# Two steps of a scan's beginning from GpSimd to VectorE, its pieces between the convolution products, and more buffers for x

## The chip, the cores and the metric

The kernel runs on one core of one Trainium2 chip. The metric is the device time of one execution in microseconds (us), the median of several runs. Short names as in the profile: PE is TensorE (PEld its weight loads), DVE VectorE, ACT ScalarE, POOL GpSimd, SP SyncE, whose queue issues all DMA transfers here.

## The reference

Input x is (4, 64, 64, 96) in fp32. Two layers hold a selective scan over the pixels (layers 0 and 1), two hold attention and a small feed-forward net (layers 2 and 3). The change concerns the scan layers only. Cut to what matters, one of them computes:

```python
x = x + conv_ref(_gn(x), ...)          # _gn: group norm, 32 groups of 3 channels

xz = einsum('bhwc,ec->bhwe', x, in_proj_w)             # 96 -> 2 * 192
xp, z = split(xz, 2)
xc = silu(depthwise_conv_3x3(xp) + conv_b)             # 192 channels
xs = [rows, columns, rows reversed, columns reversed]  # K = 4 directions over 4096 pixels
dts, B, C = split(xs @ x_proj_weight, [6, 22])         # rank 6, 16 states, 16 states
delta = softplus(dts @ dt_projs_weight + bias)
h = exp(delta * A) * h + (delta * u) * B               # scan along the pixels, u = xs
y = sum over states(h * C) + D * u
out = (layernorm(sum over directions(y)) * silu(z)) @ out_proj_w
```

## The kernel before

**Units.** A scan layer is worked on in two pairs of images, so there are four units (two layers, two pairs). The 2 x 192 channels of a pair lie in three tiles of 128 partitions (j = 0, 1, 2; tile 2 holds the last 64 channels of both images). Before each unit's scan stands a stage `between_scans` (L107), which makes the scan's inputs (`scan_inputs`, L122) and at the same time the outputs of the unit before (`scan_outputs`, L246); the first stage has no outputs to make. Both are generators: for each of the 16 groups of `scan_outputs` (256 pixels of both images) `scan_inputs` is advanced twice.

**The inputs of a scan, in program order.** `measure` (L174) for each of the two images: eight tiles xt of x, 96 x 512, are loaded by SP and go through bn_stats on DVE (L180); two tiny matmuls gm and gv (L187, L195) and a power on POOL (L81) give mean and factor of each group. `project` (L198), eight times for each image: a tile xn of x is loaded (L204), normalised on DVE (L205), multiplied on PE by in_proj (ips, three matmuls, L209); ACT copies the results into padded images img (L211, L212) or puts the gates through Silu into zs (L215, L216), which SP stores to zg. Then the 3x3 convolution, part of it on PE (`conv_product`, L147: nine matmuls cps with diagonal weights for eight rows, then Silu on ACT, L154) and part of it on DVE (`conv_chain`, L158: nine steps L167 and L169 for sixteen rows, then Silu on ACT, L170). Two chains are begun during the projection of the second image; two products stand before the scan's beginning and six products and six chains after it.

**The beginning of a scan.** `PairScan.begin` (L362) does for the first chunk of 1024 pixels what the scan does for later chunks while it runs. `project` (L373) makes B, C and the ranks of delta: six matmuls xps (L390), copies to cdt on ACT (L392), a store of cdt to crow in DRAM (L393), transposes btps (L397). B is then split into three bf16 terms, each the remainder of the one before: parts[0] on ACT (L403), rest on DVE (L404), parts[1] on ACT (L406), parts[2] on POOL (L408), transposes bpps (L412) and a copy to bparts on ACT (L416). `discretise` (L419) makes delta: matmuls dps (L434), Softplus on ACT (L438), du = delta * u on POOL (L440), transposes dups of it (L447), copies to dut on ACT (L449). Both are generators, whose yields mark places where the running scan takes up the next piece. In the stage ahead `begin` exhausts both at once:

```python
conv_product(1, 0)
conv_product(1, 8)
scan.begin(nc, pp)
yield
for n in range(2, 8):
    conv_product(*((1, 8 * n) if n < 6 else (0, 8 * n)))
```

**The order of the work.** In the stages a scheduler of the language orders each engine's instructions from their program order and its own idea of durations when the kernel is built; each engine then works through its list in order and waits where an input or a buffer isn't ready. In the scan itself (`PairScan.scan`, through `InOrder`) the program order is kept; the profile shows all that runs through that helper, the token layers not among it, as L71.

**Buffers.** Tiles with a name share a fixed number of places: two for xt and two for xn; the pool of the stage has three for what names no number. A transfer into a place waits until the tile that was there has been read. Tiles of the scan take over the memory of the stage's tiles, so its first tiles wait for the last of these.

Of the kernel before, what the change touches and what calls it, by code (L numbers as in the profile page):

```python
# [16 lines left out]
F32 = mybir.dt.float32  # L17
# [4 lines left out]
ALU = mybir.AluOpType  # L22
# [6 lines left out]
C = 96  # L29
# [46 lines left out]
def rstd_of(nc, pool, var, shape, tag, half):  # L76

    ve = pool.tile(shape, F32, name=f"{tag}_ve")
    nc.vector.tensor_scalar(ve, var, EPS, None, ALU.add)  # L79
    rs = pool.tile(shape, F32, name=f"{tag}_rs")  # L80
    nc.gpsimd.tensor_tensor(rs, ve, half, ALU.pow)  # L81
    return rs
# [39 lines left out]
def scan_inputs(tc, stage, cst, ident, half, u, scan, layer, pr):  # L122


    nc = tc.nc
    par, zg, x_src = layer.par, layer.zg[pr], layer.x_src
    pa = stage.enter_context(tc.tile_pool(name="a", bufs=1))
    p2 = stage.enter_context(tc.tile_pool(name="a2", bufs=3))
    pp = stage.enter_context(tc.tile_pool(name="a_ps", bufs=5, space=PSUM))

    wi = pa.tile([C, 2, 2 * DI], F32, name="wi")
    nc.sync.dma_start(out=wi, in_=layer.w["wi"].rearrange("i c d -> c i d"))

    diag = pa.tile([128, 9, 128], F32, name="diag")
    for tap in range(9):
        nc.gpsimd.tensor_scalar(diag[:, tap], ident, par[:, 0, P_CONV + tap : P_CONV + tap + 1], None, ALU.mult)

    imgs = []
    for j in range(3):
        img = pa.tile([128, HW + 2, HW + 2], F32, name=f"img{j}", tag=f"img{j}")  # L140
        nc.gpsimd.memset(img[:, 0], 0.0)
        nc.gpsimd.memset(img[:, HW + 1], 0.0)
        nc.gpsimd.memset(img[:, 1 : HW + 1, 0:1], 0.0)
        nc.gpsimd.memset(img[:, 1 : HW + 1, HW + 1 : HW + 2], 0.0)
        imgs.append(img)

    def conv_product(j, c):  # L147

        ps = pp.tile([128, 8, HW], F32, name="cps", tag="mm")
        for tap in range(9):  # L150
            dy, dx = divmod(tap, 3)
            v = imgs[j][:, c + dy : c + dy + 8, dx : dx + HW]
            nc.tensor.matmul(ps, diag[:, tap], v, start=(tap == 0), stop=(tap == 8))
        nc.scalar.activation(  # L154
            u[j][:, HW * c : HW * (c + 8)], ps.rearrange("p h w -> p (h w)"), AF.Silu, bias=par[:, 0, P_CB : P_CB + 1]
        )

    def conv_chain(j, c):  # L158

        s, cols = j // 2, slice(HW * c, HW * (c + 16))  # L160
        to = u[j][:, cols].rearrange("p (h w) -> p h w", w=HW)
        for tap in range(9):
            dy, dx = divmod(tap, 3)
            v = imgs[j][:, c + dy : c + dy + 16, dx : dx + HW]
            weight = par[:, s, P_CONV + tap : P_CONV + tap + 1]
            if tap == 0:
                nc.vector.tensor_scalar(to, v, weight, par[:, s, P_CB : P_CB + 1], ALU.mult, ALU.add)  # L167
            else:
                nc.vector.scalar_tensor_tensor(to, v, weight, to, ALU.mult, ALU.add)  # L169
        nc.scalar.activation(u[j][:, cols], u[j][:, cols], AF.Silu)  # L170

    norms = []

    def measure(i):  # L174

        stats = p2.tile([C, 8, 6], F32, name="stats")
        for g in range(8):
            xt = p2.tile([C, 512], F32, name="xt", bufs=2)
            nc.sync.dma_start(out=xt, in_=x_src[2 * pr + i, :, 512 * g : 512 * g + 512])
            nc.vector.bn_stats(stats[:, g], xt)  # L180
            if g % 2:
                yield
        mv = p2.tile([C, 2], F32, name="mv")
        nc.vector.bn_aggr(mv, stats.rearrange("c g s -> c (g s)"))

        gm = pp.tile([C, 1], F32, name="gm", tag="mm")
        nc.tensor.matmul(gm, cst["group"], mv[:, 0:1], start=True, stop=True)  # L187
        mean = p2.tile([C, 1], F32, name="mean")
        nc.vector.tensor_copy(mean, gm)
        dev = p2.tile([C, 1], F32, name="dev")  # L190
        nc.vector.tensor_tensor(dev, mv[:, 0:1], mean, ALU.subtract)
        spread = p2.tile([C, 1], F32, name="spread")
        nc.vector.scalar_tensor_tensor(spread, dev, dev, mv[:, 1:2], ALU.mult, ALU.add)
        gv = pp.tile([C, 1], F32, name="gv", tag="mm")
        nc.tensor.matmul(gv, cst["group"], spread, start=True, stop=True)  # L195
        norms.append((mean, rstd_of(nc, p2, gv, [C, 1], "gn", half[:C, 0:1])))

    def project(i, c):  # L198


        mine, other = slice(D1 * i, D1 * i + D1), slice(D1 - D1 * i, 128 - D1 * i)
        cols, rows = slice(512 * c, 512 * c + 512), slice(1 + 8 * c, 9 + 8 * c)
        xn = p2.tile([C, 512], F32, name="xn", bufs=2)
        nc.sync.dma_start(out=xn, in_=x_src[2 * pr + i, :, cols])  # L204
        nc.vector.tensor_scalar(xn, xn, *norms[i], ALU.subtract, ALU.mult)  # L205
        pss = []
        for q in range(3):
            ps = pp.tile([128, 8, HW], F32, name=f"ips{q}", tag="mm")
            nc.tensor.matmul(ps, wi[:, i, 128 * q : 128 * q + 128], xn, start=True, stop=True)  # L209
            pss.append(ps)  # L210
        nc.scalar.copy(imgs[i][:, rows, 1 : HW + 1], pss[0])  # L211
        nc.scalar.copy(imgs[2][mine, rows, 1 : HW + 1], pss[1][mine])  # L212
        zs = p2.tile([128, 2, 512], F32, name="zs", bufs=2)
        flat = [ps.rearrange("p h w -> p (h w)") for ps in pss]
        nc.scalar.activation(zs[other, 0], flat[1][other], AF.Silu)  # L215
        nc.scalar.activation(zs[:, 1], flat[2], AF.Silu)  # L216
        nc.sync.dma_start(out=zg[i, :, cols], in_=zs[:, 1])
        nc.sync.dma_start(out=zg[2, mine, cols], in_=zs[other, 0])

    for i in range(2):  # L220
        yield from measure(i)
    for c in range(8):
        project(0, c)
        if c % 2:
            yield

    for c in range(8):
        project(1, c)
        if c == 2:
            conv_chain(0, 0)  # L230
        elif c == 5:
            conv_chain(2, 0)
        if c % 2:
            yield
    conv_product(1, 0)
    conv_product(1, 8)
    scan.begin(nc, pp)
    yield
    for n in range(2, 8):
        conv_product(*((1, 8 * n) if n < 6 else (0, 8 * n)))  # L240
        yield
        conv_chain(*((0, 16), (0, 32), (2, 16), (2, 32), (2, 48), (1, 48))[n - 2])
        yield


def scan_outputs(tc, stage, ident, half, layer, pr, pp, turned="pt", summed="po"):  # L246
# [91 lines left out]
class PairScan:  # L338
# [22 lines left out]

    def begin(self, nc, pm):  # L362

        for _ in self.project(nc, self.pq, pm, "mm", 0, 0):
            pass
        for _ in self.discretise(nc, self.pq, pm, ("mm", "mm"), 0):
            pass

    def project(self, nc, p2, pm, tag, k, ci):  # L373


        wx = self.weights[k][0]
# [22 lines left out]
        parts = self.pq.tile([128, T // 128, 3, 2 * NS], BF16, name="parts")  # L399
        rest = self.pq.tile([128, T // 128, 2 * NS], F32, name="rest")  # L400
# [4 lines left out]
        yield 2, 10  # L405
        nc.scalar.copy(parts[:, :, 1], rest)  # L406
        yield 2, 10
        nc.gpsimd.tensor_tensor(parts[:, :, 2], rest, parts[:, :, 1], ALU.subtract)  # L408
        yield 2, 12
        ps = pm.tile([NP, T], BF16, name="bpps", tag=tag)  # L410
        for t in range(T // 128):
# [4 lines left out]
        nc.scalar.copy(bparts, ps)  # L416
        yield None

    def discretise(self, nc, p2, pm, tags, at):  # L419

        k, _, j = self.steps[at]
        uv, _, _, cdt, _ = self.projected[at // 3]
# [14 lines left out]
        for ps, cols in zip(pss, halves):  # L437
            nc.scalar.activation(delta[:, cols], ps, AF.Softplus, bias=bias)  # L438
        yield 6
        nc.gpsimd.tensor_tensor(  # L440
            du.rearrange("p (a b) -> p a b", b=HW), delta.rearrange("p (a b) -> p a b", b=HW), uv[j], ALU.mult
        )
        for hf in range(2):
# [12 lines left out]
    def scan(self, stage, nc):  # L456
# [4 lines left out]
        p2 = stage.enter_context(tc.tile_pool(name="b_2", bufs=2))  # L461

        odd = stage.enter_context(tc.tile_pool(name="b_o", bufs=1))
        pm = stage.enter_context(tc.tile_pool(name="b_ps", bufs=1, space=PSUM))

        def begin_project(k, ci):
            return self.project(nc, odd if ci % 2 else self.pq, pm, "m1", k, ci)

        def begin_discretise(at):
            return self.discretise(nc, odd if at % 2 else self.pq, pm, ("m0", "m1"), at)  # L470

        def spread(to, crow, j, row):

# [175 lines left out]
        for g, (at, n0) in enumerate(groups):  # L649
            k, ci, j = steps[at]  # L650
# [410 lines left out]
```

## Time and profile before

| What | Value |
|---|---|
| Three runs | 10762.23, 10764.9 and 10784.58 us, median 10764.9 |
| Profiled execution | 10752.09 us, of it span 10750.3 us |
| Busy over the span | PE 75%, PEld 56%, DVE 89%, ACT 82%, POOL 84% |
| Mean granted TensorE clock | 0.88 |
| DMA | 2126.70 MB, mean 198 GB/s |
| L408 parts on POOL, in the stages | 4 times, mean 5.744 us |
| L440 du on POOL, in the stages | 4 times, mean 2.345 us |
| L153 cps on PE | 576 matmul records, mean 0.594 us |
| L169 chain step on DVE | 256 times, mean 1.274 us |
| L180 bn_stats on DVE | 64 times, mean 0.682 us; 32.3 us idle before them, all for DMA xt |
| L205 xn on DVE | 64 times, mean 0.536 us; 20.6 us idle before them |

The busy shares are means over the whole span, of which the four scans take the most. The stages ahead of them have to be read on their own: by windows (busy time of each engine in a stretch), and by the timeline of an engine, in which a line gives start, duration, engine, line of the code, operation, output and inputs, and in brackets the idle time before it and what ended that. Times in the timeline count from the span's start. A matmul in fp32 leaves several records, so counts of PE in a window are more than the matmuls in the code.

### The profile page before, as it was taken

The page shows a single profiled execution, that of the slowest core. Times are in us where ns is not written, and L with a number is a line of the kernel's source. Part 1 is how long each engine was busy: PE and PEld are TensorE (multiplying, and loading weights), DVE is VectorE, ACT ScalarE, POOL GpSimd, SP SyncE. Part 2 cuts the span into 40 slices and gives each one's busy share as a digit, 9 for nine tenths or more (in the row PEclk, how much of TensorE's full clock was granted, in tenths as well). Part 3 has the DMA queues.
Part 4 walks back from the last instruction along what each step waited for, and adds up shares of the span by engine and source line. Part 5 has one row for each costly group of instructions (what it writes and reads, how often), then busy time and mean ns, then how long its engine had stood idle before and what let it go on. Part 6 is the DMA issues. An engine that isn't in the chain of part 4 may idle for free. (4 is left out here: it accounts for less than half of the span.)

```text
span 10750.3 us, 142469 instructions
## 1 busy us (share of the span) xinstructions
PE 8091.1 (75%) x47648; PEld 5985.1 (56%) x47648; DVE 9599.0 (89%) x6866; ACT 8765.2 (82%) x18779; POOL 9043.5 (84%) x5306
## 2 busy tenths in 40 slices
PE   6777777777777777776877777777777777777666
PEld 3555555554555555554455555555455555555554
DVE  6999999997899999998799999999789999999755
ACT  4888888885888888886688888888588888888666
POOL 3999999993799999997399999999379999999745
PEclk9888898988888899898888889988888888989887
DMA  3677777776577777777467777777567777777710
GB/s 111 209 209 221 215 223 221 217 212 166 183 210 214 220 220 219 217 220 201 151 206 214 215 218 222 217 220 216 152 192 208 217 221 218 219 216 221 198 43 24
DMA packets 908758, 2126.70 MB, mean 198 GB/s; under 512 B 331094, under 2 KB 640664, under 8 KB 710296
## 3 DMA queue, kind: packets, MB, share of 16 engines
q1 hardware_dynamic: 908024, 2117.59, 67.6%
q8 instruction: 378, 6.19, 0.2%
q14 instruction: 356, 2.92, 0.1%
HBM read 1955.85 MB, written 161.48 MB: 197 GB/s over the span
## 5 line engine op out<-in xcount | busy, mean ns | idle before, releaser
L71 POOL TENSOR_TENSOR h<-h,cb 128x1024 f32<-128x1024 f32 x3072 | 7193.5, 2365 | 236.5 <-issue 63.7
L71 DVE TENSOR_TENSOR_SCAN h<-da,last,bp 128x1024 f32<-128x1024 f32 x2064 | 4735.7, 2334 | 144.3 <-PE bp L71 23.2
L71 ACT ACTIVATE x<-dut,bt 128x128 f32<-128x128 f32 x12288 | 3495.0, 370 | 1.5 <-PE bp L71 1.1
L71 PE MATMUL yp<-ident,h 128*128 128x128 f32 x24576 | 3371.1, 297 | 10.2 <-POOL h L71 10.2
L71 PEld LDWEIGHTS yp<-ident,h 128*128 128x128 f32 x24576 | 3196.8, 157 | 126.1 <-issue 75.0
L71 ACT ACTIVATE da<-delta,amat 128x1024 f32<-128x1024 f32 x2752 | 3059.7, 1138 | 96.8 <-DVE h L71 95.8
L71 PE MATMUL bp<-ident,x 128*128 128x128 f32 x10240 | 1677.1, 316 | 1283.0 <-DVE h L71 919.1
L71 PEld LDWEIGHTS bp<-ident,x 128*128 128x128 f32 x10240 | 1361.3, 163 | 1839.0 <-ACT x L71 1031.1
L71 DVE TENSOR_TENSOR bp<-du,bp 128x1024 f32<-128x1024 f32 x1472 | 1778.6, 1212 | 327.7 <-PE bp L71 326.1
L71 DVE TENSOR_TENSOR_SCAN h<-da,bp 128x1024 f32<-128x1024 f32 x688 | 1537.5, 2274 | 53.3 <-ACT da L71 13.3
L71 PE MATMUL bp<-bparts,sel 96*128 96x512 bf16 x2944 | 918.3, 398 | 758.9 <-DVE h L71 741.3
L71 PEld LDWEIGHTS <-sel 96*128 96x128 bf16 x2944 | 226.8, 100 | 1554.7 <-DVE h L71 1048.9
L71 ACT ACTIVATE bp<-delta,amat 128x1024 f32<-128x1024 f32 x320 | 358.1, 1119 | 529.5 <-DVE h L71 527.7
L71 POOL TENSOR_TENSOR dbu<-du,bb 128x1024 f32<-128x1024 f32 x320 | 754.7, 2358 | 0.0
L71 POOL COPY last<-h 128x2 f32<-128x2 f32 x1152 | 216.0, 188 | 420.0 <-DVE h L71 358.9
L71 DVE TENSOR_TENSOR_SCAN h<-bp,last,dbu 128x1024 f32<-128x1024 f32 x240 | 558.5, 2327 | 9.0 <-POOL dbu L71 7.6
L71 PE MATMUL xps<-u,wx 128*76 128x512 f32 x720 | 532.9, 825 | 0.0
L81 POOL TENSOR_TENSOR ln_rs<-ln_ve,half 128x4 f32<-128x4 f32 x64 | 82.6, 1290 | 529.6 <-DVE ln_ve L79 464.2
L71 ACT ACT_TABLE_LOAD x380 | 487.5, 1283 | 23.4 <-DMA x<-xo 16.7
L71 POOL TENSOR_TENSOR du<-delta,u 128x1024 f32<-128x1024 f32 x188 | 496.4, 2640 | 0.0
L71 PE MATMUL dps<-cdt,wdt 12*128 12x512 f32 x752 | 435.8, 659 | 0.0
L71 ACT COPY ysum<-yp 128x1024 f32<-128x1024 f32 x192 | 194.5, 1013 | 294.5 <-PE yp L71 294.5
(156 smaller groups left out, 6395.0 us busy)
## 6 DMA issues: line engine op xcount, KB each, us to landing
cb<-crow SPq DMA_DIRECT2D x1024, 1024.0 KB
cb<-crow SPq DMA_DIRECT2D x1024, 512.0 KB
bb<-crow SPq DMA_DIRECT2D x384, 256.0 KB
bb<-crow SPq DMA_DIRECT2D x128, 512.0 KB
y<-ysum SPq DMA_DIRECT2D x192, 256.0 KB
kept<-y SPq DMA_DIRECT2D x160, 256.0 KB
y<-ysum SPq DMA_DIRECT2D x64, 512.0 KB
zt<-zg SPq DMA_DIRECT2D x64, 384.0 KB
```

The lines of the kernel that those rows point to most:

```text
L71: return self.tc.keep_in_program_order(getattr(self.engine, op)(*args, **kwargs))
L81: nc.gpsimd.tensor_tensor(rs, ve, half, ALU.pow)
```

## The change

Three edits, all in the stages:

- The beginning of a scan takes the engine for its two POOL steps as an argument, `free`. In the stage ahead this is DVE, in the running scan POOL as before.
- `begin` becomes a generator over the pieces of `project` and `discretise`. Four pieces are taken up after each of the six convolution products n = 2 to 7, and what is left after the last.
- xt gets four places in place of two, xn the pool's three in place of two.

```diff
         for g in range(8):
-            xt = p2.tile([C, 512], F32, name="xt", bufs=2)
+            xt = p2.tile([C, 512], F32, name="xt", bufs=4)
...
-        xn = p2.tile([C, 512], F32, name="xn", bufs=2)
+        xn = p2.tile([C, 512], F32, name="xn")
...
     conv_product(1, 0)
     conv_product(1, 8)
-    scan.begin(nc, pp)
-    yield
+    beginnings = scan.begin(nc, pp)
     for n in range(2, 8):
         conv_product(*((1, 8 * n) if n < 6 else (0, 8 * n)))
+        for _ in range(4):
+            next(beginnings, None)
         yield
         conv_chain(*((0, 16), (0, 32), (2, 16), (2, 32), (2, 48), (1, 48))[n - 2])
         yield
+    for _ in beginnings:
+        pass
...
     def begin(self, nc, pm):
-        for _ in self.project(nc, self.pq, pm, "mm", 0, 0):
-            pass
-        for _ in self.discretise(nc, self.pq, pm, ("mm", "mm"), 0):
-            pass
+        yield from self.project(nc, nc.vector, self.pq, pm, "mm", 0, 0)
+        yield from self.discretise(nc, nc.vector, self.pq, pm, ("mm", "mm"), 0)
...
-    def project(self, nc, p2, pm, tag, k, ci):
+    def project(self, nc, free, p2, pm, tag, k, ci):
...
-        nc.gpsimd.tensor_tensor(parts[:, :, 2], rest, parts[:, :, 1], ALU.subtract)
+        free.tensor_tensor(parts[:, :, 2], rest, parts[:, :, 1], ALU.subtract)
...
-    def discretise(self, nc, p2, pm, tags, at):
+    def discretise(self, nc, free, p2, pm, tags, at):
...
-        nc.gpsimd.tensor_tensor(
+        free.tensor_tensor(
             du.rearrange("p (a b) -> p a b", b=HW), delta.rearrange("p (a b) -> p a b", b=HW), uv[j], ALU.mult
         )
...
         def begin_project(k, ci):
-            return self.project(nc, odd if ci % 2 else self.pq, pm, "m1", k, ci)
+            return self.project(nc, nc.gpsimd, odd if ci % 2 else self.pq, pm, "m1", k, ci)
         def begin_discretise(at):
-            return self.discretise(nc, odd if at % 2 else self.pq, pm, ("m0", "m1"), at)
+            return self.discretise(nc, nc.gpsimd, odd if at % 2 else self.pq, pm, ("m0", "m1"), at)
```

## The prediction

> **What bounds the kernel now.** First the page's time slices. The program has four scans with a stage ahead of each, and VectorE (DVE) shows where these stages lie: the digit falls from 9 to 6, 8 or 7 in slices 1, 10, 19 and 29.
>
> ```profile
> DVE  6999999997899999998799999999789999999755
> ```
>
> The change touches only these stages. I put a stage's end at the first tensor_tensor_scan after it (198.1, 2741.2, 5281.1 and 7831.1 us in the timeline) and its start at the span's start or the last yp matmul of the scan before (2497.1, 5036.1, 7582.9). They last 198.1, 244.1, 245.0 and 248.2 us, 935 of 10750.3 us. So the most that can be gained lies in 9% of the span.
>
> Second, the stages in windows. The first stage: measuring x, projecting it, two convolution products with the products xps of the scan's beginning, the rest of the beginning, the last six convolution products. Columns: busy us (count) of PE, PEld, DVE, ACT, POOL, then clock, DMA share, GB/s.
>
> ```profile
> 12.50:42.00 29.50, 1.81 (x9) 1.55 (x9) 13.50 (x27) 0.00 (x0) 0.57 (x1) 1.00 0.32 101
> 42.00:98.50 56.50, 46.97 (x97) 18.07 (x98) 48.50 (x52) 39.45 (x67) 0.56 (x1) 1.00 0.48 154
> 98.50:120.40 21.90, 21.58 (x57) 9.02 (x55) 21.90 (x20) 5.97 (x9) 0.00 (x0) 1.00 0.06 18
> 120.40:147.50 27.10, 6.51 (x20) 3.76 (x21) 19.67 (x18) 5.63 (x9) 16.70 (x2) 0.53 0.04 10
> 147.50:195.00 47.50, 47.41 (x110) 20.65 (x109) 0.00 (x0) 7.39 (x11) 0.00 (x0) 0.98 0.00 0
> ```
>
> TensorE (PE) is full in rows 3 and 5 and nearly idle in row 4, where GpSimd (POOL) works; DVE has nothing left in row 5. The chain is PE's, with a hole. The timelines of PE and of POOL (start, duration, what; idle before and its releaser) name it:
>
> ```profile
> 137.79 1.09 PE L412 MATMUL bpps<-ident,parts 128*96 128x128 bf16 x8 [17.40 <-POOL parts L408]
> ...
> 145.78 1.97 PE L447 MATMUL dups<-ident,du 128*128 128x128 f32 x8 [3.19 <-POOL du L440]
> 147.55 47.36 PE L153 MATMUL cps<-img,diag 128*128 128x512 f32 x108
> ```
> ```profile
> 123.37 14.37 POOL L408 TENSOR_TENSOR parts<-rest,parts 128x256 bf16<-128x256 f32 x1 [80.44 <-ACT parts L406]
> ```
>
> 47.36 us of products that need nothing from the beginning stand behind it in PE's queue. Row 1 has its own limit, in DVE's timeline: after each pair of bn_stats DVE waits for the next pair of xt, as there are two buffers.
>
> ```profile
> 31.73 1.28 DVE L180 BATCH_NORM_STATS2 stats<-xt 96x6 f32<-96x512 f32 x2 [2.06 <-DMA xt<-in_x]
> 35.23 1.28 DVE L180 BATCH_NORM_STATS2 stats<-xt 96x6 f32<-96x512 f32 x2 [2.22 <-DMA xt<-in_x]
> ```
>
> Last, windows of the second stage, where scan_outputs of the pair before runs along (stages three and four look alike: projections take 79.0 and 80.2 us there).
>
> ```profile
> 2509.00:2556.40 47.40, 23.38 (x64) 13.50 (x65) 27.03 (x86) 14.84 (x34) 6.43 (x12) 0.57 0.68 196
> 2556.40:2634.20 77.80, 66.90 (x169) 32.12 (x169) 62.69 (x118) 57.29 (x110) 10.27 (x7) 0.85 0.61 183
> 2634.20:2672.20 38.00, 32.97 (x97) 16.09 (x96) 31.36 (x37) 16.99 (x28) 5.61 (x2) 0.82 0.18 49
> 2672.20:2736.60 64.40, 61.13 (x189) 31.22 (x188) 32.97 (x68) 25.32 (x52) 6.36 (x5) 1.00 0.29 83
> ```
>
> PE's clock column is below 1 wherever PE has holes, and DVE is at 81% in row 2.
>
> **What the Trainium skill says.** "GPSIMD Engine Reference", Specifications: POOL shares its SBUF interfaces with VectorE and contends with DVE instructions that have two SBUF inputs. The trace agrees: L408 took 14.37 us beside back-to-back convolution chains (L169 reads img and u), 5.74 in the mean of its four, and the same operation in the scan 0.675. "TensorE: Matmul & The Clock Gate", Part 1: an idle array falls to half clock and returns only after a few us of work. Agrees: pt x6 takes 2.00 us after a wait (at 2512.74) and 0.82 in a full stream (at 2697.16). "DMA: Bandwidth & Descriptors", Anatomy of one DMA: some 2 us fixed per transfer whatever its size; the waits of 2.06 and 2.22 us above agree.
>
> **The change, part by part.** The instruction order, fixed when the kernel is built, differs in the four stages alone; the scans and token layers have the same order.
>
> *1. parts and du on DVE.* POOL loses 4 x (5.74 + 2.35). DVE gets, per stage, 0.41 (as rest, L404, same shape) and 1.23 (as bp<-du,bp, same size): 1.6 us. DVE is idle in row 5 of stage one, so they are free there; elsewhere counted under 3.
>
> *2. Pieces handed out.* Four pieces follow each of the six last products. In PE's new order the twelve xps, btps, bpps, dps and dups matmuls stand between products, dups after the last. Stage one: PE's idle of 17.40 + 3.19 + 0.31 (before btps) goes, and the four dps matmuls run warm (3.78 us here, 2.07 in the scan): -22.6. Cost: behind the last product now come dups (1.97, warm less) and two dut copies (0.59 each) before ACT's table load and the first da, where 3.2 us passed from the last product to the scan; I take 5.0, so +1.8. SP's one crow store and the DVE steps move too: DVE's rest, parts and du stand almost last in its queue, behind them only four chain steps of 1.19 us. With the stage's new times DVE reaches rest at about 123 and PE's btps ends at 124: a wait of a us on an engine with time to spare.
>
> *3. xt from two places to four, xn from two to three.* Loop of one xt place: bn_stats 0.64, issue 0.46, landing 2.1 = 3.2 us, so 1.6 per tile with two places (measured 1.7) and 0.8 with four; 196.6 KB at the 220 GB/s of the busiest slices is 0.9. I take 0.95: first landing at 12.5 as now, 16 tiles to about 28, 1 for image 0's statistics in DVE's queue, 1.9 from the last tile to PE's first projection: 31 against 41.97, -11. The wx, wdt loads and one xn move behind xt in SP's queue; their users come later. For xn: issue 57.05, DVE 60.06, PE 60.75 to 63.56, next issue 63.59: 6.5 us per place, 3.3 per projection with two places (row 2: 56.5 / 16 = 3.5) and 2.2 with three, below PE's 2.81. So PE sets the pace: 16 x 2.81 + 2.1 for the cold start + 1 = 48, -8.5. The order bears this out: 24 chain steps stand ahead of the last xn on DVE, where 34 did, so DVE has 35 us of work in it.
>
> *Stage one:* -11 - 8.5 - 22.6 + 1.8 = **-40**.
>
> *Stages two to four.* Measuring there keeps step with scan_outputs (11 us per group: DVE, POOL's power, ACT, PE, ACT, DVE, PE, DVE in turn), not with xt. The new order starts group 4's and 5's statistics one step earlier: I take -4 (between -7 and +3, as bn_stats now stand ahead of group 2's ln_ve). Projections: 45 us of ips and four groups' pt and po at 2.7 warm = 56, with 5 of holes 61, where 77.8 went with five groups: -17, of which 3 is a group given to the next part. Convolutions: 61.8 for eight products, 10.2 for the beginning, eight groups 21.6 (two of them in the tail), 4 of holes; today 102.4 with 7.5 of holes and cold clock: with the extra group -4. Tail +1.5. Sum -23.5; DVE has 154 us of work in this stage and more of it now falls beside the products, with xo and gt of a group queued behind chain steps, rest and du, and PE's po waiting for gt. I give 5 back for that: **-18** each, between +5 and -28; -54 for three.
>
> Sum -94 against the profiled execution (10752.1, span 10750.3); the median of the runs is 10764.9, 13 above it, and I carry the difference over: **10671 us**.
>
> **The rivals.** A, the forecast, all three parts pay: -94 (-65 to -125), chance 0.68. B, *the stages with outputs keep their length*, since the chain of scan_outputs, not PE, sets them: for it speaks that x<-xo is what the scan's first da waits for (7.15 us, ACT), against it that PE has no hole between 2672 and 2727. Stage one's -40 and three times 0 to -6: -40 to -58, 10716; chance 0.20. C, *only the hole fills* (xt and xn bound by bandwidth or by ACT, which has 39.45 us in the 56.5): -21 in stage one, -4 each in the others: -33, 10732; chance 0.05. D, *slower*: DVE becomes the bound. Its rest, parts and du each hold the queue until PE has finished a product put ahead (7.7 us), and PE's po then waits for the gt behind: 23 us per stage, 69 in three, against stage one's -40: +29 (10794) or, with less hold, within the noise. It decides once a stage with outputs loses over 13 us. Against it: DVE had 33 us of work in the 64.4 of row 4. Chance 0.07, half of it under the bound. That the change doesn't do what it says is excluded by the order of instructions.
>
> **How the numbers follow.** About 0.2% (21 us) is what a measurement of this kernel can tell from no change. A, B and C lie beyond it: faster 0.93; D gives same 0.03 and slower 0.04. The range runs from A's far end with a little over, 10630, to B's weak end, 10725; C and D, 0.12, and A's extreme are left out.
>
> **What would show it.** Right: no wait of PE for parts or du above 1 us, first ips near 31, first product near 79, first scan near 158; parts on DVE at 0.4 us. Stages two to four near 226. Wrong: in these, PE idle behind DVE's gt or xn as much as now; DVE idle at rest or du by several us; the second stage still over 238 us long after its yp matmul, which is rival B.

## The result, and the profile after

| | Before | After |
|---|---|---|
| Runs | 10774.74 us, median of four (10762.23 to 10785.51) | 10669.58 us, median of four (10664.13 to 10671.99) |
| Ratio | | 0.9902, interval 0.9885 to 0.9919 |
| Profiled execution (its span) | 10752.09 us (10750.3) | 10664.13 us (10662.4) |

The change takes 105 us off, against a forecast of 94: **faster** (the interval lies wholly below 1), and inside the range. That the absolute time was met (10671 forecast) is partly luck: the gain was 11 us larger than forecast, and a fourth run moved the median of before up by 10 us.

The gain lies in the four stages. Each is measured here from the start of the last group of yp matmuls of the scan before (the first one from the span's start) to the first tensor_tensor_scan, in us. The prediction took the end of that group, which is 1.1 us later in the kernel before.

| Kernel | one | two | three | four | Sum |
|---|---|---|---|---|---|
| before | 198.1 | 245.2 | 246.2 | 249.2 | 938.7 |
| after | 151.2 | 224.0 | 222.9 | 235.1 | 833.3 |
| difference | -46.9 | -21.2 | -23.3 | -14.1 | -105.4 |

The stages lose as much as the medians, while the two profiled executions differ by 88 us only. The remaining 17.5 us are in the scans (9187.1 us before, 9195.7 after) and the token layers (624.4 and 633.4), which the change leaves alone. The section on the hardware comes back to that.

The page's time slices of DVE after the change. The dips are where they were, at slices 1, 10, 19 and 29; the scans between them look as before.

```profile
DVE  8999999997999999998899999999699999999755
```

Windows of stage one after the change (columns as in the prediction): measuring, projections, then the products in four stretches.

```profile
13.30:31.00 17.70, 1.81 (x9) 1.56 (x9) 13.49 (x28) 0.00 (x0) 0.58 (x1) 1.00 0.59 176
31.00:76.50 45.50, 44.50 (x97) 19.21 (x98) 37.12 (x42) 37.36 (x64) 0.56 (x1) 1.00 0.59 182
76.50:99.70 23.20, 23.20 (x56) 10.17 (x55) 23.20 (x21) 5.07 (x8) 0.00 (x0) 1.00 0.08 26
99.70:122.20 22.50, 22.50 (x60) 9.65 (x59) 22.50 (x20) 5.69 (x9) 0.00 (x0) 1.00 0.05 12
122.20:147.00 24.80, 24.80 (x66) 10.72 (x65) 8.26 (x9) 8.41 (x10) 0.00 (x0) 1.00 0.00 0
```

Compare each row's first number (its length) with PE's busy time. PE is full from 76.5 to 147.0 us; the row in which it had 6.51 us of work in 27.10 is gone. In the second row it is busy 44.50 of 45.50 us, where it was busy 46.97 of 56.50. The first row is 11.8 us shorter, and its DMA share is 0.59 where it was 0.32.

PE's timeline shows what stands where the hole was. Every piece of the beginning lies between products, and none of these lines has a wait in brackets until the scan's own first matmul.

```profile
120.38 0.68 PE L399 MATMUL btps<-ident,cdt 32*128 32x32 f32 x8
120.99 7.99 PE L153 MATMUL cps<-img,diag 128*128 128x512 f32 x18
128.82 0.61 PE L414 MATMUL bpps<-ident,parts 128*96 128x128 bf16 x8
129.27 7.95 PE L153 MATMUL cps<-img,diag 128*128 128x512 f32 x18
137.14 1.98 PE L436 MATMUL dps<-cdt,wdt 12*128 12x512 f32 x4
139.05 7.99 PE L153 MATMUL cps<-img,diag 128*128 128x512 f32 x18
146.88 1.04 PE L449 MATMUL dups<-ident,du 128*128 128x128 f32 x8
148.79 0.59 PE L71 MATMUL bp<-bparts,sel 96*128 96x512 bf16 x2 [0.87 <-ACT dut L451]
```

On DVE, parts and du now take 0.43 and 1.23 us in stage one. DVE is idle for 11.21 us ahead of du, until ACT has made delta: it has run out of chains by then, and nobody waits for it.

```profile
123.75 0.43 DVE L410 TENSOR_TENSOR parts<-rest,parts 128x256 bf16<-128x256 f32 x1
124.09 5.25 DVE L169 SCALAR_TENSOR_TENSOR u<-img,par,u 128x1024 f32<-128x1024 f32 x4
140.55 1.23 DVE L442 TENSOR_TENSOR du<-delta,u 128x1024 f32<-128x1024 f32 x1 [11.21 <-ACT delta L440]
```

Last, windows of the second stage: measuring, projections, products to the scan.

```profile
2463.00:2508.40 45.40, 23.85 (x71) 13.91 (x72) 27.25 (x87) 16.11 (x37) 6.59 (x12) 0.62 0.77 201
2508.40:2566.70 58.30, 54.71 (x149) 25.23 (x148) 51.02 (x88) 49.75 (x93) 4.78 (x3) 0.97 0.75 222
2566.70:2668.70 102.00, 94.45 (x298) 46.90 (x297) 76.16 (x136) 47.55 (x92) 13.04 (x8) 0.98 0.31 85
```

The projections took 77.8 us and take 58.3, and PE's clock in them rose from 0.85 to 0.97. Measuring is hardly shorter, and neither are the products, which took 38.00 + 64.40.

### The profile page after: what moved, and what is told of

It is laid out like the page before. It is cut to its first block, busy times and chain, and to the rows that moved or that the text cites. A ratio compares the mean times of both kernels' runs of the same rounds, so it can differ in the third digit from the quotient of the medians.

```text
span 10662.4 us, 142477 instructions
## 1 busy us (share of the span) xinstructions
PE 8056.0 (76%) x47648; PEld 5958.1 (56%) x47648; DVE 9606.8 (90%) x6874; ACT 8773.7 (82%) x18779; POOL 9021.4 (85%) x5298
```

## The experiments

The theory to test: separate gains, each with its place. xt's places set the pace of measuring; xn's places set that of the projections; handing out the pieces fills PE's hole. Open was whether the move to DVE has a share in that. The main rival for stages two to four was that the outputs' chain sets them.

Stage lengths of every kernel that was timed side by side with the kernel before, from one profile each:

| Kernel | one | two | three | four | Sum |
|---|---|---|---|---|---|
| e1 buffers only | 184.4 | 227.7 | 226.3 | 244.0 | 882.4 |
| e2 handing out only | 173.5 | 239.4 | 239.3 | 244.7 | 896.9 |
| e3 DVE only | 184.0 | 242.1 | 244.0 | 248.9 | 919.0 |
| e4 after, steps on POOL | 150.3 | 222.9 | 223.4 | 231.4 | 828.0 |
| e5 after, xt two places | 164.0 | 226.0 | 223.9 | 230.8 | 844.7 |
| e6 after, xn two places | 160.9 | 233.2 | 234.9 | 240.5 | 869.5 |
| e7 pieces earlier | 150.2 | 221.3 | 222.1 | 229.7 | 823.4 |
| e8 after again | 149.8 | 225.6 | 222.8 | 233.6 | 832.0 |
| e9 measuring first | 150.3 | 228.8 | 226.5 | 235.7 | 841.3 |
| e10 = e4 + e7 | 150.6 | 224.4 | 225.1 | 231.5 | 831.6 |
| e11 = e9 + e10 | 148.9 | 228.2 | 229.2 | 236.2 | 842.5 |

Two profiles of the changed kernel (after, e8) show how far to trust one: they agree within 2 us in every stage.

### e1: the kernel before with the buffers alone

```diff
-            xt = p2.tile([C, 512], F32, name="xt", bufs=2)
+            xt = p2.tile([C, 512], F32, name="xt", bufs=4)
-        xn = p2.tile([C, 512], F32, name="xn", bufs=2)
+        xn = p2.tile([C, 512], F32, name="xn")
```

> Only the places: xt four, xn three; the beginning at once, its two steps on POOL. My theory (each part of the sum stands by itself, PE's queue is the chain): first scan op at 198 - 11 (measuring) - 9 (projections) = 178 us, the PE wait for parts of about 17 us still there; projections of stages two to four down from 78 to about 60 us, each of these stages about 15 us shorter; in all -65 us. Rival, the outputs' chain sets stages two to four: only the first stage shrinks, -20 to -25 us in all. Rival, the places were bound by DMA bandwidth: under -10.

Measured: 10695.17 us against 10757.05, ratio 0.9939 (0.9927 to 0.9952), -62 us. Stage one is only 13.7 us shorter, although its first product comes 22.7 us earlier (75.77, before 98.52). PE's and POOL's timelines of this kernel show where the rest went.

```profile
122.50 1.09 PE L412 MATMUL bpps<-ident,parts 128*96 128x128 bf16 x8 [24.86 <-POOL parts L408]
131.06 1.97 PE L447 MATMUL dups<-ident,du 128*128 128x128 f32 x8 [3.77 <-POOL du L440]
```
```profile
99.46 22.98 POOL L408 TENSOR_TENSOR parts<-rest,parts 128x256 bf16<-128x256 f32 x1 [68.40 <-ACT parts L406]
```

PE's hole grew from 17.40 to 24.86 us. PE reaches the beginning earlier, when DVE has more of its chains left, and POOL's parts takes 22.98 us beside them instead of 14.37 (the section on the hardware shows what it ended with). So 9 of the 22.7 us that the buffers save are lost again before the scan, 8 of them in these two waits.

### e2: handing out alone

```diff
-            xt = p2.tile([C, 512], F32, name="xt", bufs=4)
+            xt = p2.tile([C, 512], F32, name="xt", bufs=2)
-        xn = p2.tile([C, 512], F32, name="xn")
+        xn = p2.tile([C, 512], F32, name="xn", bufs=2)
...
-        yield from self.project(nc, nc.vector, self.pq, pm, "mm", 0, 0)
-        yield from self.discretise(nc, nc.vector, self.pq, pm, ("mm", "mm"), 0)
+        yield from self.project(nc, nc.gpsimd, self.pq, pm, "mm", 0, 0)
+        yield from self.discretise(nc, nc.gpsimd, self.pq, pm, ("mm", "mm"), 0)
```

The diff is against the changed kernel.

> Only the handing out: four pieces after each product, parts and du on POOL, two places for xt and xn. My theory: the hole is one of PE's queue, not of POOL's speed; by the time btps come DVE has finished its chains, so parts on POOL takes 1 to 3 us behind a product of 7.7 us: first scan near 177 us (-21), stages two to four -4 to -6 each, in all -36 us. Rival, POOL's slowness is the cost: parts still takes some 14 us, PE waits 7 or more behind one product, in all -10 to -15 us.

Measured: 10706.72 us against 10757.05, ratio 0.9956 (0.9943 to 0.9968), -50 us. Stage one is 24.6 us shorter, the others 5.8, 6.9 and 4.5. The products of stage one start at 98.78 us, as before, and end 70.5 us later, just as in the changed kernel, though parts and du are still on POOL. POOL's timeline says why:

```profile
144.99 0.67 POOL L410 TENSOR_TENSOR parts<-rest,parts 128x256 bf16<-128x256 f32 x1 [101.61 <-ACT parts L408]
```

The same operation on the same engine takes 0.67 us, where it took 14.37. Handed out, it comes at 145 us, when DVE's chains are done (the last step ends at 139.66 us).

### e3: DVE alone

```diff
-    beginnings = scan.begin(nc, pp)
+    for _ in scan.begin(nc, pp):
+        pass
+    yield
     for n in range(2, 8):
         conv_product(*((1, 8 * n) if n < 6 else (0, 8 * n)))
-        for _ in range(4):
-            next(beginnings, None)
...
-    for _ in beginnings:
-        pass
```

Against the changed kernel, with two places for xt and xn as in e2.

> Only the engine: parts and du on DVE, the beginning still at once, two places for xt and xn. My theory: PE's 17.4 us before bpps shrink to about 4 (rest, ACT, one chain step, parts 0.4), the 3.2 before dups to about 2: first stage -14, others -3 each, in all -23 us. Rival, DVE's queue of chain steps holds the two steps back and PE waits as long: within 5 us of no change. Rival, the engine is what the whole change lives on: -40 or more.

Measured: 10739.29 us against 10757.05, ratio 0.9983 (0.9976 to 0.9989), -18 us. PE's waits in stage one:

```profile
124.15 1.09 PE L412 MATMUL bpps<-ident,parts 128*96 128x128 bf16 x8 [4.06 <-DVE parts L408]
131.27 1.97 PE L447 MATMUL dups<-ident,du 128*128 128x128 f32 x8 [2.32 <-DVE du L440]
```

17.40 + 3.19 us of waiting became 4.06 + 2.32: a latency of some us stays in the beginning on any engine, while stage one shortens by 14.1. In the other stages it brings about 3 us or less.

### e4: the changed kernel with the two steps on POOL

```diff
-        yield from self.project(nc, nc.vector, self.pq, pm, "mm", 0, 0)
-        yield from self.discretise(nc, nc.vector, self.pq, pm, ("mm", "mm"), 0)
+        yield from self.project(nc, nc.gpsimd, self.pq, pm, "mm", 0, 0)
+        yield from self.discretise(nc, nc.gpsimd, self.pq, pm, ("mm", "mm"), 0)
```

> The changed kernel with parts and du back on POOL. My theory: with the pieces between products the engine matters little: POOL's parts runs beside the last four or five chain steps, 3 to 7 us, a product of 7.7 covers it, du 2.35 instead of 1.23 is covered too: 0 to +8 us against the changed kernel, so -97 to -105 against before. Rival, POOL contends and PE waits in every stage: +20 to +40, so -65 to -85 against before.

Measured: 10652.42 us against 10757.05, ratio 0.9902 (0.9888 to 0.9915), -105 us: the whole gain, with the move undone. In the groups of this kernel the four parts take 1.07 us in the mean (5.74 before):

```profile
L410 POOL TENSOR_TENSOR parts<-rest,parts 128x256 bf16<-128x256 f32 x4 | 4.3, 1070 | 98.9 <-ACT parts L408 98.9
```

In stage one it takes 0.67 us here, although DVE still has four chain steps to do; the section on the hardware comes back to that. So once the pieces are handed out, the engine of parts and du makes no difference that these runs can tell.

### e5, e6 and e8: which buffer pays

```diff
-            xt = p2.tile([C, 512], F32, name="xt", bufs=4)
+            xt = p2.tile([C, 512], F32, name="xt", bufs=2)
```

That is e5; e6 is the changed kernel with `bufs=2` for xn; e8 is the changed kernel itself, run beside them.

> The changed kernel with xt back at two places. My theory: the first stage loses its 11 us of measuring (first scan near 162 us), stages two to four keep step with the outputs there and lose 0 to 4 us each: -85 to -94 us against before. Rival, four places feed stages two to four as well, since bn_stats stand in DVE's queue ahead of the outputs' steps: these lose 7 to 10 each, -65 to -73.

> The changed kernel with xn back at two places. My theory: the projections fall back from 45.5 to 55 us in the first stage and from 58 to about 73 in stages two to four: first scan near 160 us, the others 12 to 16 us longer each, in all -45 to -60 us against before. Rival, the outputs' chain or the order on DVE set the projections, not the places: first stage +9 and no more, -95.

> The changed kernel once more, on the same chip as the three above: -105 us against before as in its first runs; its stages at 151, 224, 223 and 235 us whatever the rest of the execution does, while the scans and the token layers differ by some us from execution to execution, in both directions.

Measured against 10759.54: e5 10666.15 us, 0.9915 (0.9901 to 0.9929), -93; e6 10702.05, 0.9947 (0.9934 to 0.9960), -57; e8 10647.04, 0.9896 (0.9882 to 0.9910), -112. Windows: measuring in e5, then the projections of stages one and two in e6.

```profile
12.50:43.04 30.54, 1.78 (x9) 1.52 (x9) 13.73 (x28) 0.00 (x0) 0.57 (x1) 1.00 0.35 106
```
```profile
29.60:86.20 56.60, 47.71 (x98) 18.32 (x99) 48.47 (x52) 39.59 (x67) 0.56 (x1) 1.00 0.49 154
2517.40:2588.10 70.70, 59.74 (x154) 27.70 (x153) 59.16 (x105) 53.22 (x100) 8.61 (x5) 0.90 0.64 195
```

The two loops are separate. With two places for xt, measuring takes 30.54 us again (17.70 in the changed kernel), and that is lost in stage one alone; the other stages are where they were. With two places for xn, stage one's projections take 56.60 us as before; stage two's take 70.70, and each of these stages loses 5 to 12 us.

### e7 and e10: the pieces earlier

```diff
-        for _ in range(4):
+        for _ in range((4, 5, 3, 7, 5, 0)[n - 2]):
             next(beginnings, None)
```

e10 has e4's edit too.

> The changed kernel with (4, 5, 3, 7, 5, 0) pieces after the six products, so that dups and dut come before the last product. My theory: the +1.8 us that I put on the tail goes: first scan at about 148.5 in place of 151.2 us, the other stages -1 to -2 each (their tail is the last two output groups): -4 to -8 us against the changed kernel, hardly to be told from none. Rival, the pieces bunched in one place make PE wait for du or parts there: 0 to +10.

> The changed kernel with parts and du on POOL and (4, 5, 3, 7, 5, 0) pieces. My theory: the handing out alone fills PE's hole, the engine doesn't matter (parts under 2 us on POOL once DVE's chains are done, du 2.35 behind a product): stages as with the pieces earlier or 1 to 2 us shorter, -2 to -10 us against the changed kernel. Rival, du on POOL now stands right ahead of dups with only one product between: +2 to +5.

Measured: e7 10654.07 us against 10759.54, 0.9900 (0.9886 to 0.9914); e10 10646.31 against 10751.54, 0.9899 (0.9884 to 0.9914), -105 us each. Neither can be told from the changed kernel. In e7's timeline dups stands ahead of the last product, but PE then waits for the Silu of that product (0.78 us, L154) where it waited for dut (0.87 us): one wait stands in for the other.

### e9 and e11: the next unit's statistics ahead of the outputs

```diff
-            for _ in outs:
-                for _ in range(2):
+            for g, _ in enumerate(outs):
+                for _ in range(4 if g < 2 else 1 + g % 2):
                     next(ins, None)
```

e11 adds this to e10. It gives the two images' statistics to the first two groups of outputs, and the groups taken out of measuring to later steps.

> The changed kernel with another pace in between_scans: four steps of the inputs for each of the first two output groups, then one and two in turn, so that measuring takes two groups and not four. My theory: in stages two to four measuring keeps step with the output groups (45 us for four, PE at half clock and half idle), so halving it brings the projections 20 us forward, and outputs fill PE later: stages 12 to 25 us shorter each, -40 to -70 us against the changed kernel. Rival, the chain of 16 output groups at 11 us each is itself the length of the stage (176 us and the ends): -10 to 0. The first stage is unchanged.

> e9 and e10 together. If both theories hold the gains add up, -45 to -80 us against the changed kernel, 10570 to 10610 in all; if the outputs' chain holds the stages, as e10 alone.

Measured: e9 10652.78 us against 10751.54, 0.9908 (0.9891 to 0.9924), -99; e11 10654.08, 0.9909 (0.9894 to 0.9923), -97. The expected 40 to 70 us did not come, and stages two to four are up to 5 us longer than in the changed kernel in e9 and up to 6 in e11. PE's timeline of e9 in stage two:

```profile
2484.93 2.07 PE L209 MATMUL ips<-xn,wi 96*128 96x512 f32 x2 [0.20 <-DVE xn L205]
...
2552.79 1.87 PE L209 MATMUL ips<-xn,wi 96*128 96x512 f32 x2 [5.20 <-DVE ymv L279]
...
2566.14 23.34 PE L153 MATMUL cps<-img,diag 128*128 128x512 f32 x54
```

This stage began at 2441.65 us (last yp), in the changed kernel at 2449.32. So the projections begin 43.3 us into the stage, 15.8 earlier than there (59.1), yet the first product comes after 124.5 us, 7.2 later (117.3). PE's groups between first projection and first product show why, e9 first, then the changed kernel (columns: records, busy us and mean ns, then idle before and its releasers):

```profile
L209 PE MATMUL ips<-xn,wi 96*128 96x512 f32 x96 | 51.4, 665 | 10.3 <-DVE ymv L279 6.8 <-DVE xn L205 1.8 <-ACT ys L286 1.2
L310 PE MATMUL po<-gt,wo 128*96 128x256 f32 x48 | 12.0, 395 | 3.1 <-DVE gt L303 3.1
```
```profile
L209 PE MATMUL ips<-xn,wi 96*128 96x512 f32 x96 | 45.3, 616 | 2.4 <-DVE xn L205 2.4
L310 PE MATMUL po<-gt,wo 128*96 128x256 f32 x33 | 8.2, 387 | 0.4 <-DVE gt L303 0.4
```

In e9 six groups of outputs (48 records of po) stand among the projections where four stood (33), and PE waits ahead of these two lines 13.4 us, for ymv, xn, ys and gt, where it waited 2.8. The groups left out of measuring come along later with their waits. That fits the rival that the outputs' chain is what sets the pace there; what of that chain would have to be shortened was not tried.

### e12: what starves POOL

The kernel before with each chain step that adds to u replaced by two that read one input. It leaves out the sum over the taps on DVE.

```diff
-                nc.vector.scalar_tensor_tensor(to, v, weight, to, ALU.mult, ALU.add)
+                for _ in range(2):
+                    nc.vector.tensor_scalar(to, v, weight, None, ALU.mult)
```

> The kernel before, with each chain step that adds to u replaced by two products of img alone, leaving out the sum (so u is only the last tap's product): DVE is as busy behind the beginning, but with one SBUF input. If POOL is starved by DVE's two-input steps alone, parts in the first stage takes 1 to 2 us in place of 14.4 and PE's wait falls to about 4; if any stream of DVE steps starves it (these run in the fast form, 0.8 us for 1024 elements), parts still takes 8 us or more. Time in all not compared.

Measured: 10752.25 us, once; this time is not compared. Windows that are exactly POOL's parts in stage one, in the kernel before, in e1 and in e12:

```profile
123.37:137.74 14.37, 0.00 (x0) 0.00 (x0) 14.34 (x13) 0.00 (x0) 14.37 (x1) 0.50 0.00 0
```
```profile
99.46:122.44 22.98, 0.00 (x0) 0.00 (x0) 22.95 (x21) 1.06 (x1) 22.98 (x1) 0.50 0.00 0
```
```profile
120.26:145.57 25.31, 0.00 (x0) 0.00 (x0) 25.27 (x39) 0.00 (x0) 25.31 (x1) 0.51 0.00 0
```

In all three DVE works beside POOL without a gap but for 0.03 or 0.04 us, PE has nothing, and ACT one copy at most. With steps of one input, parts takes 25.31 us, not less. So a DVE instruction need not have two inputs to do this. These steps are the fast kind: 0.744 us for 1024 elements where L169 takes 1.274. The Trainium skill ("GPSIMD Engine Reference", Specifications) names two conditions for contention, two SBUF inputs or a 2-port mode. e12 rules out that the first is the only one; the second would cover its steps if they run in such a mode, which no run here shows. A slow step with one input was not tried.

## Why the prediction was right

**Measuring, stage one: -11.** The first ips came at 30.97 us (31 forecast) against 41.97: -11.0. e5 shows that it is xt's places.

**Projections, stage one: -8.5.** They went from 56.5 to 45.5 us: -11. The loop over xn's places was the right mechanism, as e6 shows. The sum's term of 48 was too large in the work, 16 x 2.81 = 45: 2.81 us is the duration of one projection alone, and in a row they come faster. In PE's timeline the 35 records after the first five projections take 15.26 us, so 2.6 us for each six; the slow beginning, counted with 2.1 us, did come and cost about 2.8.

```profile
30.97 15.90 PE L209 MATMUL ips<-xn,wi 96*128 96x512 f32 x30
47.16 15.26 PE L209 MATMUL ips<-xn,wi 96*128 96x512 f32 x35 [0.29 <-DVE xn L205]
```

**The hole: -22.6, tail +1.8.** From first product to first scan 99.6 us became 74.7, -24.9 against a forecast -20.8. From the end of the last product to the scan it is 4.2 us (5.0 taken, 3.2 before), and 3 us more than counted went from the rest. Of these, 1.97 us are dups: the sum added them behind the last product and did not take them off ahead of it. Stage one: -46.9 for -40, as these errors all have one sign. The wait of a us at rest did not come: DVE goes into it at 122.23 us without idling, 1.2 us after btps ended.

**parts and du: free.** Right (0.43 and 1.23 us, where 1.6 were taken), and the gain was rightly put down to the handing out. What the prediction did not see is that the move can be left out. It had both numbers, 14.37 us for parts beside the chains and 0.675 in the scan, but not the conclusion that handing out takes parts away from the place where it is slow (e2, e4).

**Stages two to four: -18 each.** They lost 21.2, 23.3 and 14.1, -58.6 for -54. The sum is met better than its terms. By parts in stage two: from the last yp to the first ips 60.5 to 59.1 us, -1.4 where -4 was forecast; projections 77.7 to 58.3, -19.4 for -17; the rest 107.0 to 106.7, nothing where -2.5 was forecast and 5 given back for DVE's queue. About half of what the projections gained is PE's pace and not its waits: the matmuls ips of this stage keep PE busy for 45.3 us where it was 54.4.

The wait for which the 5 us were given back did come. These are PE's groups po from the first projection to the scan, before and after (columns as in e9):

```profile
L307 PE MATMUL po<-gt,wo 128*96 128x256 f32 x96 | 25.2, 404 | 1.3 <-DVE xo L309 0.9 <-DVE gt L300 0.4
```
```profile
L310 PE MATMUL po<-gt,wo 128*96 128x256 f32 x96 | 24.9, 405 | 5.5 <-DVE gt L303 4.6 <-DVE xo L312 0.9
```

PE waits for gt 4.6 us where it waited 0.4, 4.3 of them among the products; in stages three and four it is 4.7 and 2.7, in place of 0.4 and 0.7. The steps moved to DVE are not the reason: with them on POOL (e4) it is 4.4 us in stage two. So one of the signs that the prediction named for being wrong, PE idle behind gt or xn as much as now, came in stage two (7.0 us, 7.1 before), though the stage lost 21 us: the waits moved from xn to gt, while the wait for parts (4.2 us), waits for ys and PE's slow pace went.

Stage four gained less: its projections went from 80.0 to 70.1 us only, and the rest from 109.9 to 105.5. Windows of the projections of stages three and four, after the change:

```profile
5031.20:5087.20 56.00, 52.90 (x148) 24.53 (x147) 50.54 (x88) 49.44 (x93) 4.78 (x3) 1.00 0.77 230
7550.40:7620.50 70.10, 63.44 (x201) 32.97 (x202) 54.42 (x92) 53.92 (x102) 6.75 (x5) 0.86 0.68 194
```

PE is idle for 6.7 us in stage four and 3.1 in stage three, and its clock is 0.86 instead of 1.00: an ips takes 683 ns in the mean instead of 595, which is 8 us of the 14 between the two rows (96 records). The slow ones stand in the first 5.6 us and, after waits of 0.67 and 1.70 us close together, in the 6.1 us from 7570.4; the clock is 0.50 in both stretches. The Trainium skill ("TensorE: Matmul & The Clock Gate", Part 1), as the prediction used it, says that an idle array falls to half clock and needs some us of work to return. That is seen here, though the page gives an idle window of about 3.4 us and these two waits are 2.4 us in sum.

But the waits alone don't decide it. After one of 1.65 us at 7587.80 no ips is slow, and in e5 the same projections took 61.6 us at a clock of 0.97, an ips 610 ns, although PE was idle for 5.9 us. The outputs of that stage's layer have other matmuls (L318, L319, L321), but e5 has them too, so they are not a sufficient reason. Why stage four falls into the slow pace in one kernel and not in the other is open. "Stages three and four look alike" was read from their lengths in the kernel before, where both had gaps and a clock of 0.85 and 0.87.

So the mechanisms were right, and the terms that were off are the projections (11 for 8.5, 19.4 for 17), the hole (3 us more) and measuring in the later stages (1.4 for 4). Rival B (-40 to -58) is excluded by the stages' own lengths (second stage 224.0 us; B's mark was 238), though e9 suggests its chain as the next limit. C and D did not come.

What each part brings alone: -62 (e1), -50 (e2), -18 (e3), which is more than the -105 together. e2 and e3 fill the same hole. e1 and e2 support each other: their stages alone gave -56.3 and -41.8, and together (e4) -110.7. In stage one that is -47.8 for -38.3, since handing out also removes the longer hole that the buffers open there; stage four has 8 us more as well and stages two and three 5 less, which no run explains.

## What to carry to other kernels

When an engine waits in its queue, read what stands behind the waiting instruction; if that is independent, deal the waiting chain's pieces out between it before making the chain itself faster. Size buffers by their loop: the time round one place (6.5 us for xn) over the pace of the engine that should set it (2.81 us), rounded up, gives the number of places (three; two cost 36 us in stage lengths, e6). And test the parts of a change apart and together: a faster stage ahead can lengthen the wait behind it (e1), and a part that looks necessary (the move to DVE) can bring nothing beside another.

## What the runs showed of the hardware

**POOL beside a busy DVE.** The same POOL operation (128x256) took 0.67 us with DVE quiet, and 14.37, 22.98 and 25.31 us beside 13, 21 and 39 back-to-back DVE instructions: 21 to 38 times as long. The Trainium skill ("SBUF — State Buffer", Who interferes with whom) tells of a port pair that is held for one whole instruction while the other engine blocks. Here POOL was not let in at the end of one instruction; it lasted over many of them. In each case it ended while DVE's run still went on, so it was not shut out to the end of that either.

The traces show where it ended. In these runs each DVE step starts 0.07 to 0.09 us before the one ahead of it ends, up to one step that starts 0.04 us after that. In all three cases POOL's operation ended 0.5 us after the start of that step, which itself took 0.3 us longer than its neighbours. In the kernel before (POOL ended at 137.74 us; a timeline merges equal steps, so each line is from a window of its own):

```profile
135.94 1.27 DVE L169 SCALAR_TENSOR_TENSOR u<-img,par,u 128x1024 f32<-128x1024 f32 x1
137.24 1.58 DVE L169 SCALAR_TENSOR_TENSOR u<-img,par,u 128x1024 f32<-128x1024 f32 x1
```

In e1 the step began at 121.95 us and POOL ended at 122.44, in e12 at 145.08 and 145.57. In e4's stage one, parts came 0.1 us before such a step:

```profile
122.91 0.67 POOL L410 TENSOR_TENSOR parts<-rest,parts 128x256 bf16<-128x256 f32 x1 [92.16 <-ACT parts L408]
123.01 1.65 DVE L169 SCALAR_TENSOR_TENSOR u<-img,par,u 128x1024 f32<-128x1024 f32 x1
```

It took 0.67 us with DVE's last four chain steps still to come, and the same in e10 and e11. So what went with the long times in stage one was not that DVE was busy, but that its steps overlapped. POOL does not make the gaps: e3, without a POOL step there, has them in its last four chain steps too. This is read from six traces that agree, and no run changed the gaps alone. Why they begin where they do is open, and a gap is not the only way in: in stages two to four of the kernel before, parts ended after 2.07 to 3.27 us beside DVE steps of several kinds that all overlapped.

**Scatter where nothing changed.** The scans, whose code no run changes, took 2291 to 2307 us each in all fourteen profiles, and the token layers 624 to 633. That is why two profiled executions can differ by 88 us where the medians differ by 105: read a change of this size in its stages, not in two spans.
